# An attention and feed-forward layer on one core: weights read without copies, v's products in wider matmuls, and softmax sums over single tiles

## The chip, the cores and the metric

The kernel runs on one core of a Trainium2 chip. The metric is the device time of one execution in microseconds (us), lower is better. The median of three runs of the kernel before is 2360.73 us (2359.38 to 2362.85). A separate, profiled execution gives the trace that is read below.

## The reference

The layer works on x of 2 x 2048 rows with C = 1024 columns, all in float32:

```
x = x + attn(layernorm(x))        # one head of d = 256, keys over all 2048 rows
x = x + ffn(layernorm(x))

attn:  qkv = x @ Wqkv + bqkv;  p = softmax(q k^T / 16);  out = p v @ Wo + bo
ffn:   shared = relu(x @ up_w)^2 @ down_w                 # 1024 -> 2048 -> 1024
       routed = ((x @ fc1_w) @ expert_w) * (sum of the two largest of x @ gate_w) @ fc2_w
       layernorm(shared + routed) * gamma + beta
```

## The kernel before, in words

**Numbers.** Matmul operands are in a reduced float32 form. To keep accuracy, every operand is a pair: `hi`, the rounded value, and `lo`, what the rounding left. A product is three matmuls, hi x hi, lo x hi and hi x lo, added up in one PSUM tile (`Pass3`, L117 to L138, whose matmul is at L130). A split into hi and lo is a copy on ScalarE and a subtraction on VectorE (L142 and L143), now and then on GpSimd.

**Stages.** The 4096 rows are eight blocks of 512 rows, four for each batch element.

1. *Start* (`begin`, L458 to L520). `expert_w` is transposed on TensorE (tile `pt`, L480) and multiplied with `fc2_w` into the folded weight `fc2e` (tile `pf`). The first block of x is normalised and transposed on TensorE (L326) between the four quarters of the second of these products. The loads go through SyncE's queue.
2. *q, k and v* (`qkv_block`, L408). For each block come four v tiles (`v_tile`, L418: 128 rows x 256 columns, eight chunks of C, three matmuls each: tile `pv`) and four chunks of q and k (tile `pq`, 512 columns). Meanwhile the next block is normalised and transposed: a VectorE transpose of 32 x 32 tiles, a store to DRAM (`xt_d`), and a fetch in another order (`xt`), both on GpSimd's queue.
3. *Attention* (L712 to L763). For each of eight query blocks: scores of 16 key chunks (`ps`), the maximum, `softmax` (L581) in eight steps of two chunks, values (`po`), then `finish` (L611) and `project` (L632, tile `pw`). `softmax` adds the exponentials into a tile `sum` of 128 x 1024, two halves for the even and the odd chunks; `finish` sums over the 128 partitions and the two halves with matmuls of one column against a column of ones (tile `psum`, L622): four row tiles times two halves, 8 matmuls to a query block in the program. The trace shows each of them as two records, 16 to a query block and 128 in all.
4. *Feed-forward* (L1033 to L1290). For each of four pairs of blocks: 70 pieces of the up stage (`pu`) and 70 of the down stage (`pd`), in a scheme of seven products in place of eight (`p1` to `p7`), whose right sides are quarters of the weights or sums of quarters. A piece takes twelve matmuls. `stage` (L797) issues a piece's load on SyncE's queue into the second half of a tile `w`, `cast_piece` (L829) makes its hi on ScalarE, `end_piece` (L836) its lo on VectorE in place, and, for some pieces, stores the pair to DRAM (`w_p`, on GpSimd's queue), from where later blocks load it without a split. The pieces run about five ahead of their use; there are seven `w` tiles.

**Copies and sums of weights.** Sums of quarters are made by DMA alone: a copy of one quarter to a DRAM tile `wt` (L391), then accumulating DMAs (L399). `COPIES` lists 14 such copies: eight are the first terms of sums, six are plain copies of a quarter (three of `up_w`, three of `down_w`) so that all pieces come from tiles. `sum_step` issues one copy and perhaps one sum. It is called after blocks 4, 5 and 6 of the q, k and v stage, and at two points of each query block from the second on. A copy of a quarter with its part of `fc1_w` or `fc2e` is 2.5 MB.

**Order.** The start, the first seven q, k and v blocks and the feed-forward run in the order that the program writes (`manual_schedule`). For the eighth block and the attention a planner orders each engine's instructions by its own costs and by when their inputs are due; it may pull feed-forward instructions ahead into the end of the attention. `Norm(1)`, the second block's normalisation for the first pair, is spread over up pieces m = 0 to 13; its products `p4` start at m = 20.

Of the kernel before, what the change touches and what calls it, by code (L numbers as in the profile page):

```python
# [9 lines left out]
FP = mybir.dt.float32  # L10
# [15 lines left out]
def kernel(  # L26
# [353 lines left out]

    FIRST = {1: (0, 1), 2: (1, 1), 3: (0, 1), 4: (1, 0)}
    SUMS = [(s, q) for s in range(2) for q in (1, 3, 2, 4)]
    COPIES = SUMS + [(s, q) for s in range(2) for q in ((0, 0), (1, 0), (1, 1))]
    ADDS = dict(zip((4, 5, 6, 8, 9, 10, 11, 13), SUMS))
    last = [None]

    def sum_step(i):

        s, q = COPIES[i]
        for o, t in zip(sum_tile(s, q), quarter(s, *FIRST.get(q, q))):  # L390
            nc.gpsimd.dma_start(out=o, in_=t)  # L391
        if i in ADDS:
            s, q = ADDS[i]
            if q % 2:
                terms = quarter(s, *((0, 0) if q == 1 else (1, 1)))
            else:
                terms = sum_tile(s, q // 2)
            for o, t in zip(sum_tile(s, q), terms):
                nc.gpsimd.dma_start(out=o, in_=t, accum_op=ALU.add, max_dma_last_dim=4096)  # L399
# [8 lines left out]
    def qkv_block(n, wqkv, xT, parts, after):  # L408
# [9 lines left out]
        def v_tile(t):  # L418
            pm = bank(psa, "pv")
            if t % 2 == 0:  # L420
                got["v"] = half("v")
            acc = Pass3(pm[:, :D], NCC)
            for c in range(NCC):
                acc.add(x_chunk(xT, c, ts(t, P)), piece(wqkv[2], c, D, slice(0, D)))
            vt = got["v"][:, ts(t % 2, D)]
            nc.vector.tensor_tensor(vt, pm[:, :D], bv_sb, ALU.add)
            flush()
            split_late(vt, *(hl(units["v"])[:, s, ts(t, D)] for s in range(2)))
# [29 lines left out]
    def begin(wqkv, xT):  # L458
# [16 lines left out]

        eh, el = unit("eh"), unit("el")
        for mc in range(NLC):
            pt = bank(psc, "pt")
            for lc in range(NLC):
                nc.tensor.transpose(pt[:, ts(lc, P)], ew[:, ds(lc * LAT + mc * P, P)], ident)  # L480
            split(pt, eh[:, ts(mc, LAT)], el[:, ts(mc, LAT)])

# [25 lines left out]
        for t in range(NB):  # L508
            if t + 1 < NB:
                stats.append(row_stats(first[t + 1]))  # L510
            normalise(first[t], stats[t])
            if t == 0:
                f2hl = split_f2(1, nc.gpsimd)
            elif t == 2:
                wqkv[2] = split_unit(*ws[2], nc.gpsimd)
        r = [folded(0, accs)]
        r.append(folded(1, fold(f2hl, lambda t: transpose_tile(first[t], t, xT))))
# [63 lines left out]
    def softmax(n, j):  # L581

        s = st[n]
        s["p"].append(unit(f"p{n}_{j}"))
        e = s["s"][j // 2][:, ts(j % 2, C)]
        hi, lo = (hl(s["p"][j])[:, i, :] for i in range(2))
        e2 = e.rearrange("p (k n) -> p k n", n=W)
        mb = s["mb"].unsqueeze(1).to_broadcast([P, 2, W])
        nc.vector.tensor_tensor(e2, e2, mb, ALU.subtract)
        nc.scalar.activation(e, e, AF.Exp, scale=SC)  # L590
        split(e, hi, lo)
        if j == 0:
            s["e0"] = e
        elif j == 1:
            s["sum"] = row(f"sum{n}")
            nc.vector.tensor_tensor(s["sum"], s["e0"], e, ALU.add)
        else:
            nc.vector.tensor_tensor(s["sum"], s["sum"], e, ALU.add)
# [12 lines left out]
    def finish(n):  # L611
# [8 lines left out]
        for t in range(NB):  # L620
            for i in range(2):
                nc.tensor.matmul(  # L622
                    pt[:, t : t + 1],
                    lhsT=s["sum"][:, ds(i * W + t * P, P)],
                    rhs=ones,
                    start=i == 0,
                    stop=i == 1,
                )
# [63 lines left out]
    with tc.manual_schedule():  # L692
        norm, fold = begin(wqkv, xT)
        x3 = lambda: None
        steps = list(range(len(COPIES)))
        for i in range(NBLK - 1):
# [6 lines left out]
            if i >= NBLK // 2:  # L703
                sum_step(steps.pop(0))
# [81 lines left out]
    UPS = [up_order(4 if b == 0 else 1) for b in range(NBLK // 2)]  # L786
# [6 lines left out]
    def source(s, q, i):  # L793
        t, j = (tsum[s, q][0], i) if i < HU // P else (tsum[s, q][1], i - HU // P)
        return t[:, ts(j, P)].rearrange("(c p) i -> p c i", p=P) if s == 0 else t[ts(j, P), :]

    def stage():  # L797
# [3 lines left out]
        if len(pieces) < LATE and early:  # L801
            staged.append((early.pop(0), False, None))
            return
        n_w[0] += 1
        w = (wk if n_w[0] % 7 else wv).tile([P, 2 * W], FR, tag="w", name="w")
        if (s, p, i) in kept:
            nc.sync.dma_start(out=w.bitcast(FP), in_=kept[s, p, i])
            staged.append((w, False, None))
            return
        nc.sync.dma_start(out=as_piece(f32(w)[:, W : 2 * W], s), in_=source(s, RIGHT[p], i))  # L810
# [7 lines left out]
        staged.append((w, True, (s, p, i) if keep else None))  # L818
# [10 lines left out]
    def cast_piece():  # L829

        w, raw, key = staged.pop(0)
        if raw:
            nc.scalar.copy(w[:, 0:W], f32(w)[:, W : 2 * W])  # L833
        cast.append((w, raw, key))

    def end_piece():  # L836

        w, raw, key = cast.pop(0)
        if raw:
            v = f32(w)  # L840
            nc.vector.tensor_tensor(w[:, W : 2 * W], v[:, W : 2 * W], v[:, 0:W], ALU.subtract)  # L841
# [191 lines left out]
    with tc.manual_schedule():  # L1033
        for b in range(NBB):
# [72 lines left out]
            for m, (p, i) in enumerate(UPS[b]):  # L1107
# [229 lines left out]
```

## Time and profile before

| | |
|---|---|
| median of three runs | 2360.73 us |
| the profiled execution | 2357.94 us |
| its span on the core | 2355.8 us |
| TensorE matmul busy | 2323.3 us |
| VectorE busy | 1501.8 us |
| ScalarE busy | 1168.1 us |
| GpSimd busy | 285.4 us |
| moved by DMA | 572.54 MB, mean 243 GB/s |
| mean granted TensorE clock | 0.997 |

The span runs from the first to the last instruction. The profiled execution's own time is 2.1 us longer than its span, for what lies around it. A matmul's record lasts longer than the distance to the next one's start, since matmuls overlap; the distance is what counts against the time. Busy shares are averages over stages; which engine sets the time is read stage by stage.

| stretch, us | stage |
|---|---|
| 0 to 39.3 | start |
| 39.3 to 310.7 | q, k and v, eight blocks |
| 310.7 to 767 | attention |
| 767 to 2355.8 | feed-forward, four pairs |

### The profile page before, as it was taken

The numbers are of one execution on the slowest core, as the hardware profiler recorded it, in microseconds if no ns is written. First come the engines' busy times: TensorE is split into PE (matmuls) and PEld (weight loads), VectorE is DVE, ScalarE is ACT, GpSimd is POOL, SyncE is SP. The second block draws the span as 40 slices with busy tenths as digits, with TensorE's granted clock in tenths as the row PEclk, the third lists the DMA queues.
The fourth block names the chain that finished last, engine by engine and source line by source line (L and its number), as shares of the span: only waits on it lengthen the run. The fifth ranks groups of instructions, "written<-read, shape, count | busy, mean of one in ns | idle before, by whom it ended". The sixth has DMA issues, their size and how long they took to land.

```text
span 2355.8 us, 29360 instructions
## 1 busy us (share of the span) xinstructions
PE 2323.3 (99%) x10704; PEld 1919.4 (81%) x10704; DVE 1501.8 (64%) x2238; ACT 1168.1 (50%) x1916; POOL 285.4 (12%) x425
## 2 busy tenths in 40 slices
PE   8999999999999999999999999999999999999997
PEld 7888888888887778788788888878888877888886
DVE  5566559888877575797645577753456683435656
ACT  6555455555544643667552374743055564214245
POOL 3232111011110110111110011110000021000001
PEclk9999999999999999999999999999999999999999
DMA  5977884999997766786897789786567589665674
GB/s 197 318 256 276 286 205 127 296 315 323 286 253 211 250 208 191 228 276 209 265 316 242 229 297 319 229 267 227 193 204 278 194 267 331 189 191 187 204 247 134
DMA packets 222208, 572.54 MB, mean 243 GB/s; under 512 B 18368, under 2 KB 80320, under 8 KB 220016
## 3 DMA queue, kind: packets, MB, share of 16 engines
q1 hardware_dynamic: 152160, 315.67, 39.9%
q0 software_dynamic: 69904, 255.00, 36.1%
q8 instruction: 85, 1.39, 0.2%
q14 instruction: 59, 0.48, 0.1%
HBM read 430.61 MB, written 197.66 MB: 267 GB/s over the span
## 4 chain that ended last, share of the span: by engine, by line
PE 91%; DMA 3%; issue 3%; DVE 1%; ACT 1%; POOL 0%; SPq 0%; POOLq 0%; DVEq 0%; ACTq 0%
PE pu L130 31%; PE pd L130 28%; PE po L130 7%; PE pq L130 7%; PE ps L130 7%; PE pv L130 4%; PE pw L130 4%; DMA w<-wt 2%; PE pg L890 1%; PE pf L130 1%; PE psum L622 1%; DMA xt<-xt_d 0%; DVE w L841 0%; DMA ew<-in_L_ffn_expert_w_dram 0%; DMA res<-x 0%
## 5 line engine op out<-in xcount | busy, mean ns | idle before, releaser
L130 PE MATMUL pd<-w,sp 128*128 128x512 f32 x3336 | 759.0, 389 | 4.9 <-DVE y L1274 4.8
L130 PEld LDWEIGHTS pd<-w,sp 128*128 128x128 f32 x3336 | 625.5, 188 | 137.3 <-ACT nm L260 6.0
L130 PE MATMUL pu<-xh,w 128*128 128x512 f32 x2240 | 692.8, 390 | 0.1
L130 PEld LDWEIGHTS pu<-xh,w 128*128 128x128 f32 x2240 | 419.2, 188 | 89.9 <-DVE w L841 1.5
L130 PE MATMUL pu<-xl,w 128*128 128x512 f32 x1120 | 436.2, 389 | 0.9 <-DVE xl L150 0.9
L841 DVE TENSOR_TENSOR w<-w 128x512 fp32r<-128x512 f32 x280 | 191.6, 687 | 99.0 <-ACT w L833 92.0
L833 ACT CAST w<-w 128x512 fp32r<-128x512 f32 x280 | 170.9, 615 | 166.2 <-DMA w<-wt 155.6
L130 PEld LDWEIGHTS pu<-xl,w 128*128 128x128 f32 x1120 | 210.2, 188 | 45.1 <-DVE xl L150 1.4
L1077 ACT CAST sp<-h 128x512 fp32r<-128x512 f32 x238 | 146.3, 618 | 151.9 <-PE pd L130 125.6
L1082 DVE TENSOR_TENSOR sp<-h,sp 128x512 fp32r<-128x512 f32 x238 | 162.9, 687 | 68.1 <-ACT sp L1077 67.9
L130 PE MATMUL po<-p,v 128*128 128x512 f32 x768 | 194.3, 391 | 0.6 <-DVE p L143 0.6
L130 PE MATMUL ps<-q,k 128*128 128x512 f32 x768 | 192.5, 390 | 1.5 <-DVE max L565 1.5
L130 PEld LDWEIGHTS ps<-q,k 128*128 128x128 f32 x768 | 143.6, 188 | 31.8 <-DVE max L565 1.9
L130 PEld LDWEIGHTS po<-p,v 128*128 128x128 f32 x768 | 143.0, 188 | 30.2 <-DVE p L143 1.0
L150 DVE TENSOR_TENSOR xl<-xt,xh 128x512 fp32r<-128x512 f32 x108 | 74.4, 689 | 134.9 <-ACT xh L149 134.9
L1027 ACT ACTIVATE h<-h 128x1024 f32<-128x1024 f32 x48 | 50.7, 1055 | 208.8 <-DVE h L1137 159.8
L560 ACT COPY s<-ps 128x512 f32<-128x512 f32 x128 | 75.0, 587 | 133.5 <-PE ps L130 133.4
L213 DVE STREAM_TRANSPOSE xblk<-xrow 128x1024 f32<-128x1024 f32 x60 | 121.1, 2018 | 9.6 <-ACT xrow L283 9.6
L844 POOL DMA_DIRECT2D w_p<-w x115 | 61.6, 536 | 508.7 <-DVE w L841 435.0
L565 DVE TENSOR_TENSOR max<-ps,max 128x512 f32<-128x512 f32 x120 | 82.4, 687 | 36.3 <-ACT s L560 36.1
L130 PE MATMUL pq<-xha,w_h 128*128 128x512 f32 x256 | 99.7, 389 | 0.0
L130 PE MATMUL pq<-xha,w_l 128*128 128x512 f32 x256 | 99.7, 389 | 0.0
(181 smaller groups left out, 3031.8 us busy)
## 6 DMA issues: line engine op xcount, KB each, us to landing
w<-w_p SPq DMA_DIRECT2D x280, 512.0 KB, 4.2
w<-wt SPq DMA_DIRECT2D x280, 256.0 KB, 3.4
w_p<-w POOLq DMA_DIRECT2D x115, 512.0 KB, 4.6
xt_d<-xblk POOLq DMA_DIRECT2D x56, 512.0 KB, 4.4
xt<-xt_d POOLq DMA_DIRECT2D x56, 512.0 KB, 6.7
wt<-in_L_ffn_up_w_dram POOLq DMA_DIRECT2D x9, 2048.0 KB, 23.8
wt<-in_L_ffn_down_w_dram POOLq DMA_DIRECT2D x9, 2048.0 KB, 31.1
xres<-in_L_attn_x_dram SPq DMA_DIRECT2D x32, 512.0 KB, 11.2
```

The source lines that it names most:

```text
L130: nc.tensor.matmul(self.ps, lhsT=a, rhs=b, start=self.i == 0, stop=self.i == self.n - 1, skip_group_check=self.on,)
L150: late_ops.append(lambda: nc.vector.tensor_tensor(lo, t, f32(hi), ALU.subtract))
L213: nc.vector.transpose(b.rearrange("p (q k i) -> p q k i", q=P // SQ, i=SQ), r.rearrange("p (k i q) -> p q k i", k=NCC, i=SQ),)
L560: nc.scalar.copy(s["s"][k // 4][:, ts(k % 4, W)], pm)
L565: nc.vector.tensor_tensor(s["max"], pm, s["max"], ALU.max)
L622: nc.tensor.matmul(pt[:, t : t + 1], lhsT=s["sum"][:, ds(i * W + t * P, P)], rhs=ones, start=i == 0, stop=i == 1,)
L833: nc.scalar.copy(w[:, 0:W], f32(w)[:, W : 2 * W])
L841: nc.vector.tensor_tensor(w[:, W : 2 * W], v[:, W : 2 * W], v[:, 0:W], ALU.subtract)
L844: nc.gpsimd.dma_start(out=kept[key], in_=w.bitcast(FP))
L1027: nc.scalar.activation(o, v, AF.Relu)
L1077: nc.scalar.copy(t[:, 0:W], v)
L1082: add(t[:, W : 2 * W], v, f32(t)[:, 0:W], ALU.subtract)
```

## The change: what it does

- **v's weights side by side.** For each chunk of C the hi and lo columns of v's weights lie next to each other, 512 wide. One matmul multiplies x's hi by both, one of 256 columns x's lo by hi. VectorE adds the two halves of the PSUM tile, in one instruction more to a tile. The weights are split in two halves, one after the other, beside the second product of the start, with their subtraction on GpSimd.
- **Halves of sums.** In the last step of `softmax`, VectorE adds the two halves of `sum` and then the two halves of the last exponentials, so `finish` has one matmul to a row tile.
- **Fewer copies, sums in single terms.** The three quarters of `up_w` and `fc1_w` are no longer copied; their pieces load from the inputs, into a tile of the pool `spp` (`raw`), except for the first four pieces of `p1`, which come from a copy `lead` of 1 MB. `sum_step` issues one term, a copy or an accumulation: two in the start, 14 in the attention, one in the first up stage at m = 46. The copies of `down_w`'s three quarters move to m = 16, 26 and 36 of the first up stage. None is left in the q, k and v stage.
- **TensorE kept awake.** Transposes of the identity into an unused PSUM tile: 3 ahead of the first transposes, 14 ahead of the third group, 5 after the last.
- **An earlier second block.** The eleven steps of `Norm(1)` come at m = 0 to 11 in place of 0 to 13, and the splits for `p4` start at m = 11 in place of 13.

```diff
+    SECOND = {1: (0, 0), 2: 1, 3: (1, 1), 4: 2}
     SUMS = [(s, q) for s in range(2) for q in (1, 3, 2, 4)]
-    COPIES = SUMS + [(s, q) for s in range(2) for q in ((0, 0), (1, 0), (1, 1))]
-    ADDS = dict(zip((4, 5, 6, 8, 9, 10, 11, 13), SUMS))
+    LEAD = 4
+    STEPS = [(a, 0) for a in SUMS[:3]]
+    for a, c in zip(SUMS, SUMS[3:] + [None] * 3):
+        STEPS += ([(c, 0)] if c else []) + [(a, 1)]
+    STEPS.insert(3, None)
+    lead = dram.tile([HC, LEAD * P], FP, name="wt_lead")
...
     def sum_step(i):
+        if STEPS[i] is None:
+            nc.gpsimd.dma_start(out=lead, in_=up_w[0:HC, 0 : LEAD * P])
+            return
+        (s, q), second = STEPS[i]
+        a = (SECOND if second else FIRST)[q]
+        terms = quarter(s, *a) if isinstance(a, tuple) else sum_tile(s, a)
+        for o, t in zip(sum_tile(s, q), terms):
+            if second:
+                nc.gpsimd.dma_start(out=o, in_=t, accum_op=ALU.add, max_dma_last_dim=4096)
+            else:
+                nc.gpsimd.dma_start(out=o, in_=t)
+
+    def copy_step(q):
+        for o, t in zip(sum_tile(1, q), quarter(1, *q)):
             nc.gpsimd.dma_start(out=o, in_=t)
...
-            acc = Pass3(pm[:, :D], NCC)
             for c in range(NCC):
-                acc.add(x_chunk(xT, c, ts(t, P)), piece(wqkv[2], c, D, slice(0, D)))
+                xh, xl = x_chunk(xT, c, ts(t, P))
+                w = wqkv[2][c // 4].rearrange("p (c n) -> p c n", n=2 * D)[:, c % 4]
+                ops = [(pm, xh, w), (pm[:, :D], xl, w[:, :D])]
+                for i, (o, x_, w_) in enumerate(ops[:: 1 if c + 1 < NCC else -1]):
+                    nc.tensor.matmul(
+                        o,
+                        lhsT=x_,
+                        rhs=w_,
+                        start=c + i == 0,
+                        stop=c == NCC - 1 and i == 1,
+                        skip_group_check=True,
+                    )
             vt = got["v"][:, ts(t % 2, D)]
             nc.vector.tensor_tensor(vt, pm[:, :D], bv_sb, ALU.add)
+            nc.vector.tensor_tensor(vt, pm[:, D : 2 * D], vt, ALU.add)
...
+        def busy(n):
+            pt = bank(psb, "busy")
+            for _ in range(n):
+                nc.tensor.transpose(pt[:, 0:P], ident, ident)
+
         eh, el = unit("eh"), unit("el")
+        busy(3)
         for mc in range(NLC):
+            if mc == 2:
+                busy(14)
...
+        busy(5)
...
-            elif t == 2:
-                wqkv[2] = split_unit(*ws[2], nc.gpsimd)
         r = [folded(0, accs)]
-        r.append(folded(1, fold(f2hl, lambda t: transpose_tile(first[t], t, xT))))
+        wqkv[2] = []
+
+        def beside(t):
+            transpose_tile(first[t], t, xT)
+            if t < 2:
+                sum_step(steps.pop(0))
+            if t in (1, 2):
+                u = unit(f"w2_{t}")
+                uv = u.rearrange("p (c n) -> p c n", n=2 * D)
+                wv = ws[2][1].rearrange("p (c n) -> p c n", n=D)[:, ts(t - 1, NCC // 2)]
+                split(wv, uv[:, :, 0:D], uv[:, :, D : 2 * D], nc.gpsimd)
+                wqkv[2].append(u)
+
+        r.append(folded(1, fold(f2hl, beside)))
...
+        last = j == NKC // 2 - 1
+        if last:
+            half_sum = s["sum"][:, 0:W]
+            nc.vector.tensor_tensor(half_sum, half_sum, s["sum"][:, W:C], ALU.add)
         nc.vector.tensor_tensor(e2, e2, mb, ALU.subtract)
...
+        elif not last:
+            nc.vector.tensor_tensor(s["sum"], s["sum"], e, ALU.add)
         else:
-            nc.vector.tensor_tensor(s["sum"], s["sum"], e, ALU.add)
+            for i in range(2):
+                nc.vector.tensor_tensor(half_sum, half_sum, e[:, ts(i, W)], ALU.add)
...
         for t in range(NB):
-            for i in range(2):
-                nc.tensor.matmul(
-                    pt[:, t : t + 1],
-                    lhsT=s["sum"][:, ds(i * W + t * P, P)],
-                    rhs=ones,
-                    start=i == 0,
-                    stop=i == 1,
-                )
+            nc.tensor.matmul(
+                pt[:, t : t + 1], lhsT=s["sum"][:, ts(t, P)], rhs=ones, start=True, stop=True
+            )
...
-            if i >= NBLK // 2:
-                sum_step(steps.pop(0))
...
+    def direct(s, p, i):
+        return s == 0 and p in ("p1", "p2", "p3") and (p, i // LEAD) != ("p1", 0)
+
+    def source(s, p, i):
+        q = RIGHT[p]
+        if s == 0 and isinstance(q, tuple):
+            parts = quarter(s, *q) if direct(s, p, i) else [lead]
+        else:
+            parts = tsum[s, q]
...
-        nc.sync.dma_start(out=as_piece(f32(w)[:, W : 2 * W], s), in_=source(s, RIGHT[p], i))
+        if direct(s, p, i):
+            raw = spp.tile([P, 2 * W], FP, tag="sp", name="raw")[:, 0:W]
+        else:
+            raw = f32(w)[:, W : 2 * W]
+        nc.sync.dma_start(out=as_piece(raw, s), in_=source(s, p, i))
...
-                if b == 0 and m in (0, 1, 2, 4, 6, 8, 9, 10, 11, 12, 13):
+                if b == 0 and m in (0, 1, 2, 3, 4, 6, 7, 8, 9, 10, 11):
                     norm2.step()
...
+                if b == 0 and m in (16, 26, 36):
+                    copy_step(((0, 0), (1, 0), (1, 1))[m // 10 - 1])
+                elif b == 0 and m == 46:
+                    sum_step(steps.pop(0))
-                m4 = 12 if b == 0 else 10
+                m4 = 10
```

More of the change, by code (lines that the diff above doesn't have):

```diff
@@ L381 @@
     FIRST = {1: (0, 1), 2: (1, 1), 3: (0, 1), 4: (1, 0)}
+    SECOND = {1: (0, 0), 2: 1, 3: (1, 1), 4: 2}
     SUMS = [(s, q) for s in range(2) for q in (1, 3, 2, 4)]
-    COPIES = SUMS + [(s, q) for s in range(2) for q in ((0, 0), (1, 0), (1, 1))]
-    ADDS = dict(zip((4, 5, 6, 8, 9, 10, 11, 13), SUMS))
+    LEAD = 4
[4 more added lines that the diff above has]
+    lead = dram.tile([HC, LEAD * P], FP, name="wt_lead")
     last = [None]
     def sum_step(i):
-        s, q = COPIES[i]
-        for o, t in zip(sum_tile(s, q), quarter(s, *FIRST.get(q, q))):
-            nc.gpsimd.dma_start(out=o, in_=t)
[L392 to L399, printed above, removed]
+        if STEPS[i] is None:
[11 more added lines that the diff above has]
+        for o, t in zip(sum_tile(1, q), quarter(1, *q)):
+            nc.gpsimd.dma_start(out=o, in_=t)
     kv = {}
@@ L692 @@
     with tc.manual_schedule():
+        steps = list(range(len(STEPS)))
         norm, fold = begin(wqkv, xT)
         x3 = lambda: None
-        steps = list(range(len(COPIES)))
         for i in range(NBLK - 1):
@@ L784, in up_order @@
         return order + [(p, i) for p in ("p4", "p6", "p5", "p3", "p7") for i in range(NK)]
-    UPS = [up_order(4 if b == 0 else 1) for b in range(NBLK // 2)]
+    UPS = [up_order(LEAD if b == 0 else 1) for b in range(NBLK // 2)]
     DOWN = [(p, i) for p in ("p1", "p2", "p6", "p5", "p3", "p7", "p4") for i in range(NK)]
@@ L791 @@
     LATE = 5
-    def source(s, q, i):
-        t, j = (tsum[s, q][0], i) if i < HU // P else (tsum[s, q][1], i - HU // P)
+    def direct(s, p, i):
[6 more added lines that the diff above has]
+            parts = tsum[s, q]
+        t, j = (parts[0], i) if i < HU // P else (parts[1], i - HU // P)
         return t[:, ts(j, P)].rearrange("(c p) i -> p c i", p=P) if s == 0 else t[ts(j, P), :]
@@ L801, in stage @@
         if len(pieces) < LATE and early:
-            staged.append((early.pop(0), False, None))
+            staged.append((early.pop(0), None, None))
             return
@@ L807, in stage @@
             nc.sync.dma_start(out=w.bitcast(FP), in_=kept[s, p, i])
-            staged.append((w, False, None))
+            staged.append((w, None, None))
             return
-        nc.sync.dma_start(out=as_piece(f32(w)[:, W : 2 * W], s), in_=source(s, RIGHT[p], i))
+        if direct(s, p, i):
[3 more added lines that the diff above has]
+        nc.sync.dma_start(out=as_piece(raw, s), in_=source(s, p, i))
         if s == 1 and p in ("p3", "p7", "p4"):
@@ L817, in stage @@
             keep = b == 1 or i % 2 == 0
-        staged.append((w, True, (s, p, i) if keep else None))
+        staged.append((w, raw, (s, p, i) if keep else None))
     early, n_w = [], [0]
@@ L831, in cast_piece @@
         w, raw, key = staged.pop(0)
-        if raw:
-            nc.scalar.copy(w[:, 0:W], f32(w)[:, W : 2 * W])
+        if raw is not None:
+            nc.scalar.copy(w[:, 0:W], raw)
         cast.append((w, raw, key))
@@ L838, in end_piece @@
         w, raw, key = cast.pop(0)
-        if raw:
-            v = f32(w)
-            nc.vector.tensor_tensor(w[:, W : 2 * W], v[:, W : 2 * W], v[:, 0:W], ALU.subtract)
+        if raw is not None:
+            nc.vector.tensor_tensor(w[:, W : 2 * W], raw, f32(w)[:, 0:W], ALU.subtract)
         if key:
```

## The prediction

> **What bounds the kernel now.** I read the busy times first, then the chain of work that ended last, then the waits of TensorE, then single stretches.
>
> ```profile
> PE 2323.3 (99%) x10704; PEld 1919.4 (81%) x10704; DVE 1501.8 (64%) x2238; ACT 1168.1 (50%) x1916; POOL 285.4 (12%) x425
> PE 91%; DMA 3%; issue 3%; DVE 1%; ACT 1%; POOL 0%; SPq 0%; POOLq 0%; DVEq 0%; ACTq 0%
> ```
>
> The second line should not be trusted alone, and neither should 99%: matmul records overlap. So I took the distance from each matmul's start to the next one's: their sum is 2338.5 us; 3.7 us lie before the first matmul and 13.6 us after the last one's start, which makes the span of 2355.8. Taking the usual distance for each kind (227 ns for 512 columns, 120 ns for 256) leaves some 26 us of the 2338.5 as stalls. TensorE's instruction stream sets the time almost everywhere, so an instruction taken from TensorE counts in full, and one put on another engine counts only where that engine is late. The waits of TensorE say where:
>
> ```profile
> PE pt L480 <- DMA ew<-in_L_ffn_expert_w_dram: 7.2, 2, 3.7
> PE pd L130 <- DVE y L1274: 4.8, 3, 2.0
> PE pv L130 <- ACT xha L142: 2.2, 1, 2.2
> PE ps L130 <- DVE max L565: 1.5, 1, 1.5
> ...
> PE pu L130 <- DVE xl L150: 0.9, 1, 0.9
> ```
>
> (us in total, times, longest). Nothing here is large; the change can win little from waits and must win from instruction count.
>
> **1. The sums of softmax.** In the chain in order of time, these are v and q/k of one block, and the sums of one query block (start, us, what):
>
> ```profile
> 39.43 11.51 PE pv L130 x96
> 50.94 21.79 PE pq L130 x96
> ...
> 436.18 1.68 PE psum L622 x16
> ```
>
> Sixteen records take 1.68 us, 105 ns each, on TensorE's path eight times. Half go: 8 x 0.84 = **6.7 us off**. In exchange VectorE gets a 512-wide add for the halves (about 0.69, from the 512-wide `max` rows) and two 512-wide adds in place of one of 1024 (2 x 0.61 against 1.14 start to start), some 0.8 us per query block. In the steady state VectorE is busy about eight tenths and the last add is six steps of values ahead of `finish`: nothing. In the last query block, where no scores run, VectorE is full:
>
> ```profile
> 745.00:755.00 10.00, 10.00 (x46) 8.28 (x45) 10.00 (x11) 5.50 (x7) 4.07 (x6) 1.00 1.04 285
> ```
>
> (us, TensorE, its weight loads, VectorE, ScalarE, GpSimd, clock, DMA share, GB/s) and the timeline has, at its end:
>
> ```profile
> 756.69 1.23 DVE L598 TENSOR_TENSOR sum<-sum,s 128x1024 f32<-128x1024 f32 x1 [0.53 <-ACT s L590]
> 757.83 1.22 DVE L143 TENSOR_TENSOR p<-s,p 128x1024 fp32r<-128x1024 f32 x1
> ...
> 759.14 1.84 PE L622 MATMUL psum<-ones,sum 128*128 128x1 f32 x16
> ```
>
> The sum ends at 757.9 and is used at 759.14: 1.2 us to spare. TensorE comes 0.84 us earlier (the block before has lost its sums too) and VectorE 0.8 us later: 0.4 us late, and `p`'s lo behind it as much. I count **0.6 us lost**, bounded by 0 (the planner fills in up-stage matmuls, as it does at 756.64) and 1.6.
>
> **2. v's products.** A 256-column matmul costs 11.51/96 = 119.9 ns, a 512-column one 21.79/96 = 227.0. Three of the first become one of each: 359.7 becomes 346.9, 12.8 ns off, times 8 chunks x 32 tiles: **3.3 us off**. The added VectorE instruction is 0.41 us (the row of L426) times 32; VectorE works 154.8 of 271 us in this stage and four PSUM banks stand between it and TensorE: nothing. Its weights are ready in time: ScalarE's two halves (half of 1.92 us each) follow the transposes of tiles 1 and 2 at about 30 and 34 us, GpSimd's two subtractions (half of 4.62 us) end near 33.5 and 37, v starts at 39.3. If that cover of 2 us were gone it would cost what it is late.
>
> **3. Awake.** The first products run at half clock:
>
> ```profile
> 9.11 1.94 PE L480 MATMUL pt<-ident,ew 128*128 128x128 f32 x8 [3.49 <-DMA ew<-in_L_ffn_expert_w_dram]
> 12.24 0.79 PE L130 MATMUL pf<-f2h,eh 128*128 128x512 f32 x1 [1.19 <-ACT f2h L142]
> 13.69 0.63 PE L130 MATMUL pf<-f2h,eh 128*128 128x512 f32 x1
> 15.95 0.39 PE L130 MATMUL pf<-f2h,eh 128*128 128x512 f32 x1
> ```
>
> From 12.24 to 15.4 the distance is 0.43 us in place of 0.227, 7 times, and 0.36 more at the first: 1.8 us. The granted clock turns full at 15.6. With a full clock before 12 the transposes of the last groups are quicker too, and 0.2 us could come from there: 2.0 at most. The 22 added transposes at 0.21 us fit: 14 take 3.0 us of the 3.5 us wait, 5 take 1.1 of the 1.2 before 12.24. Against it stands the Trainium skill, TensorE: Matmul & The Clock Gate, Part 4 (PE-mode transpose): full clock does not engage for transposes, which do not count as busy in the same way. By that rule the gain is 0. The row of eight transposes (1.94 us in the last 3.1 us before the matmuls) did not raise the clock, but it filled too little of the time to decide. I take the middle, **1.0 us off**.
>
> **4. The pair's second block, earlier.** At 831.7 the first matmul of `p4` with a lo waits 1.1 us for `xl` (the wait of 0.9 above and its start-up). Its split comes two pieces, 5.4 us, earlier, and the eleven normalisation steps with their SyncE row loads, VectorE transposes and GpSimd stores and fetches too, into a stretch where ScalarE works 6.0 to 6.5 of 10 us, out of one (805 to 815) where it works 9.9: **1.1 us off**.
>
> **5. Copies and sums.** They are DMAs from GpSimd's queue, and cost only through what they delay. The price of a pair (2.5 MB): in the stage of q, k and v the `q_d` store issued at 204.4 lands after 9.1 us, at 213.5, and the pair issued behind it lands after 14.6 and 15.7, at 221.2. So 8 us by itself; the Trainium skill, DMA: Bandwidth & Descriptors (Queues, rings and completion order), adds that an engine consumes one ring in order and takes turns between the rings of several queues. So SyncE's loads lose half their rate while a copy lasts, and GpSimd's own transfers wait for all of it. By the page's limit of memory, 358 GB/s for a core, 5.2 MB read and written would take 15 us. I use the row, 8 us, where little else runs, and 15 where other loads run.
>
> *In the start*, two pairs are issued at about 26 to 29 us, behind GpSimd's 6 us of `f2l`. SyncE has some 2 MB to come; `w1` lands near 40 instead of 33 and its split on ScalarE starts at 41.9. The copies end near 29 + 16 + 6 = 51; the first `xt_d` is issued at 52.35, so it and the fetches behind it lose 0 to 3 us (by the page's rate the copies end near 64: see the second rival). The last fetch of a block lands 0.4 us after the next block begins and is used three v tiles, 8.6 us, later. Nothing.
>
> *In the eighth block* TensorE stalls at 278.0 for `xha`, with a slower clock behind it: 5.0 us in excess of the usual distances. The last fetch was issued at 270.5 and took 7.7 us (4.4 in the block before). The removed copy of the sixth block had landed by 254.5, so the delay comes from SyncE's own loads of `q_d` and `Wo`, which stay: 0, up to 5.0 off if I misread this.
>
> *In the attention* there are fewer transfers; they were hidden.
>
> *In the first up stage* three pairs and one accumulated pair are put ahead of `w_p` stores. A store is issued two pieces ahead of use (of which a piece is 2.72 us), its tile's next load five pieces ahead of a use seven later. Behind a 15 us copy issued at m = 16, the store of piece 20 lands at about m = 22.3; the load of piece 27 wants the tile at m = 22. Loads here took up to 9.3 us without a stall over 0.3. Nothing.
>
> *Direct pieces* load as many bytes in the same 512-byte runs; `raw` frees the load from waiting for `w`, ScalarE's copy waits for it instead, one piece later. The fifth load must wait for the memory of v's last units (about 752 us), where the kernel before issued five loads from 705.6 on; SyncE's queue holds fetches of x and residual loads at 730 to 743, which I expect the planner to put ahead. Nothing; 5 to 11 us lost if it does not.
>
> **Sum.** -6.7 + 0.6 - 3.3 - 1.0 - 1.1 = -11.5 us. Against the profiled execution's 2357.94 that is 2346.4; the median of the runs lies 2.8 us above it, so **2349.2 us**, 0.49% less. This kernel's runs tell a change from none at about 0.2%, 4.7 us.
>
> **The rivals.**
>
> *The eighth block's stall goes too.* For it: a 2.5 MB copy was in that queue in each of the three blocks. Against: landed by 254.5. Time: 2349.2 - 5.0 = 2344.2. Chance 0.10.
>
> *Late tiles in the second and third block.* The start's copies, then the fold's stores and the next rows, keep GpSimd's queue late until a fetch lands over 3 us late, as in the eighth block. Each such block costs its 5.0: 2354.2 to 2359.2. For it: the margin of 1 us at 52.35. Chance 0.12.
>
> *SyncE held by the fifth load.* Four x fetches and four residual loads issued at 752 to 756 instead of 730 to 743 leave TensorE with some values and two PSUM banks of projection: 5 to 11 us, near 2357. Against: readiness is what the planner orders by. Chance 0.06.
>
> *VectorE becomes the bound of the attention.* If every query block loses the added 0.7 us, 5.6 go: 2354.8. Against: two tenths idle. Chance 0.03.
>
> *Slower: stores behind copies.* In the attention such copies and sums took 31 to 45 us to land. If one takes 31 us in the up stage, the store of piece 20 lands at m = 28, the load of 27 comes at 28 and its split at 29.7: 2.7 pieces, 7.4 us late, in each of three copies, and as much for the sum: 30 - 11.5, 2368. It decides from about 20 us of holding on. Against: DMA is 0.66 busy here, 0.90 in the attention. Chance 0.08.
>
> **How the numbers follow.** The forecast has 0.61: 2345 to 2353 (the bounds of part 3, and of the last query block). Faster by over 0.2%, under 2356: the forecast, the first rival, half of the second, most of the third, the fourth, 0.82. Slower by over 0.2%, over 2365.4: 0.09, the last rival and a little for two at once. Within: 0.09. The range 2342 to 2358 leaves out the slow rival and the second's worse half, and a little below.
>
> **What would show it.** `psum` x64 and 0.84 us in each row of the chain; `pv` with 256 matmuls of 512 columns, 11.1 us a block; full clock by 12 us or again at 15.6; no wait for `xl` at the start of `p4`; the wait for `xha` at about 265. Wrong, if TensorE waits for `xt`, for `w` in pieces 27 to 35, or for x near 757.

## The result and the profile after

The kernel became slower: 2377.85 us (median of six runs, 2374.69 to 2382.04) against 2361.36 us of the kernel before beside it (six runs, 2358.23 to 2362.94). The ratio is 1.0073, with a 95% interval of 1.0060 to 1.0086. The prediction was 2349.2 us. The profiled execution took 2374.69 us, with a span of 2372.9 us, 17.1 us more than before.

The page of the changed kernel, its busy times and its chain by engine:

```profile
PE 2323.3 (98%) x10406; PEld 1902.8 (80%) x10406; DVE 1520.5 (64%) x2286; ACT 1167.5 (49%) x1917; POOL 281.0 (12%) x421
PE 78%; DMA 8%; issue 5%; DVE 4%; ACT 2%; POOL 1%; SPq 1%; POOLq 0%; DVEq 0%; ACTq 0%
```

TensorE has 298 records fewer, as foreseen, and DMA went from 3% to 8% of the chain. The waits of TensorE (us in total, times, longest):

```profile
PE ps L130 <- DVE max L610: 10.9, 2, 10.6
PE pd L130 <- DVE y L1335: 4.8, 3, 1.7
PE pu L130 <- DVE w L898: 4.7, 3, 3.1
PE pv L439 <- ACT xha L142: 4.6, 2, 4.3
PE pu L130 <- ACT w L891: 3.2, 1, 3.2
...
PE pq L130 <- DVE v L449: 1.4, 2, 1.3
```

Four new or larger waits stand out: one of 10.6 us for the maximum of the scores, two for weights in the up stage (3.2 and 3.1), one of 4.3 us at the last block of q, k and v. The next table puts each at its place. It takes the start of one kind of matmul in both traces as a mark, and lists how much later (+) or earlier (-) it comes after the change.

| stretch, by the start of | time in before, us | gained or lost, us |
|---|---|---|
| span's start to the first block's q and k | 0 to 50.8 | -2.0 |
| to the third block's q and k | to 117.4 | +2.1 |
| to the seventh block's q and k | to 250.6 | -0.6 |
| to the eighth block's q and k | to 288.7 | +1.9 |
| to the sixth query block's `psum` | to 665.4 | -4.7 |
| to the seventh query block's `psum` | to 724.7 | +10.9 |
| to piece 4 of the up stage | to 783.0 | -1.6 |
| to piece 30 | to 862.0 | +1.9 |
| to piece 60 | to 943.8 | +9.9 |
| to the end | to 2355.8 | -0.6 |
| sum (unrounded) | | +17.1 |

The gains on TensorE are there. Two losses, of 11 and 10 us, outweigh them.

**The loss in the attention.** The timelines of SyncE's queue, ScalarE, VectorE and TensorE in the changed kernel show the wait of 10.6 us and what ended it (start, us, what, idle time before it and what ended that):

```profile
701.43 11.45 SPq L868 DMA_DIRECT2D w<-wt_lead  x4
...
716.84 0.62 ACT L891 CAST w<-w 128x512 fp32r<-128x512 f32 x1 [14.81 <-DMA w<-wt_lead]
717.37 0.58 ACT L605 COPY s<-ps 128x512 f32<-128x512 f32 x1
...
718.10 0.68 DVE L610 TENSOR_TENSOR max<-ps,max 128x512 f32<-128x512 f32 x1
...
718.84 2.93 PE L130 MATMUL ps<-q,k 128*128 128x512 f32 x6 [10.63 <-DVE max L610]
```

Beside these loads GpSimd's queue moves a copy and a sum of weights; the sum was issued at 689 us and its larger part lands 29 us later. The first load of 256 KB of feed-forward weights takes 15.4 us, the other three about 20. The first piece that uses such a load starts at 758.7 us, but the planner has put its copy to hi (L891) into ScalarE's stream ahead of the copy of a score tile (L605), so the attention waits for it. Around these waits TensorE's granted clock falls too (stretch, TensorE busy, its loads, VectorE, ScalarE, GpSimd, clock, DMA share, GB/s):

```profile
713.00:723.00 10.00, 4.16 (x10) 3.29 (x11) 3.21 (x4) 3.35 (x6) 0.00 (x0) 0.50 0.93 209
...
938.00:948.00 10.00, 6.39 (x14) 4.73 (x15) 4.23 (x7) 7.69 (x11) 0.53 (x1) 0.51 0.48 156
```

**The loss in the up stage.** The timeline there shows the accumulation that is issued at m = 46, and what a piece then waits for:

```profile
916.54 1.96 POOL L404 DMA_DIRECT2D wt<-wt  x2
...
937.85 0.62 ACT L891 CAST w<-raw 128x512 fp32r<-128x512 f32 x1 [18.49 <-DMA raw<-in_L_ffn_up_w_dram]
938.52 0.80 PE L130 MATMUL pu<-xh,w 128*128 128x512 f32 x1 [3.20 <-ACT w L891]
...
942.40 0.79 PE L130 MATMUL pu<-xh,w 128*128 128x512 f32 x1 [3.09 <-DVE w L898]
```

**Why a load of 256 KB takes 13 to 20 us.** A "packet" is here what the profile counts as one: a run of 512 or of 4096 bytes in these loads and sums. The DMA view of the changed kernel for 918 to 936 us (packets, MB, share of the 16 engines' time; then issues with the median us to landing):

```profile
DMA packets 1623, 4.01 MB, mean 223 GB/s; under 512 B 78, under 2 KB 729, under 8 KB 1622
...
q0 software_dynamic: 952, 3.66, 94.9%
q1 hardware_dynamic: 670, 0.33, 8.2%
...
raw<-in_L_ffn_up_w_dram SPq DMA_DIRECT2D x4, 256.0 KB, 16.0
...
wt<-wt POOLq DMA_DIRECT2D x1, 512.0 KB, 19.6
```

and of the kernel before for the same stretch of time, where no sum runs:

```profile
q1 hardware_dynamic: 3652, 1.81, 34.4%
q0 software_dynamic: 359, 1.34, 20.9%
...
w<-wt SPq DMA_DIRECT2D x6, 256.0 KB, 3.1
```

The engines are full, and SyncE's queue (q1) gets 0.33 of 4.01 MB: 8%, not half. The packet counts tell why. A piece of weights is read in runs of 512 bytes, 512 packets a load; the accumulation (q0) moves packets of 4096 bytes. In part of the stretch q1 moves nothing. From 925 to 933 us both queues have work all the time:

```profile
q0 software_dynamic: 363, 1.42, 94.5%
q1 hardware_dynamic: 354, 0.18, 11.3%
```

That is one packet of each in turn, and 11% of the bytes for q1. In the attention, from 706 to 718 us, the counts are 585 and 585. From the shares, a packet of q0 holds an engine 0.945 x 16 x 8 / 363 = 0.33 us, one of q1 0.113 x 16 x 8 / 354 = 0.041 us. 354 packets in 8 us make 11.6 us for the 512 of a load. Before that a load waits for its turn to begin: the one issued at 921.00 us moves its first packet 3.5 us later, where one of the kernel before (issued at 924.76) needs 1.0 us. That load took 16.8 us. A piece is used every 2.72 us, and five pieces of lead, 13.6 us, don't cover it. What is shared evenly is turns, not bytes.

### The profile page after: what moved, and what is told of

The parts are those of the page before. It is cut to its first block, busy times and chain, and to the rows that moved or that the text cites. A ratio compares the mean times of both kernels' runs of the same rounds, so it can differ in the third digit from the quotient of the medians.

```text
span 2372.9 us, 28742 instructions
## 1 busy us (share of the span) xinstructions
PE 2323.3 (98%) x10406; PEld 1902.8 (80%) x10406; DVE 1520.5 (64%) x2286; ACT 1167.5 (49%) x1917; POOL 281.0 (12%) x421
## 4 chain that ended last, share of the span: by engine, by line
PE 78%; DMA 8%; issue 5%; DVE 4%; ACT 2%; POOL 1%; SPq 1%; POOLq 0%; DVEq 0%; ACTq 0%
PE pu L130 30%; PE pd L130 28%; PE po L130 7%; PE ps L130 7%; PE pw L130 4%; DMA w<-wt 2%; DMA xt_d<-xblk 2%; DVE xblk L213 1%; PE pg L947 1%; DMA w<-in_L_attn_Wqkv_dram 1%; PE pq L130 1%; DMA w<-wt_lead 1%; DMA raw<-in_L_ffn_up_w_dram 1%; DVE xla L143 1%; DMA xt<-xt_d 1%
## 5 line engine op out<-in xcount | busy, mean ns | idle before, releaser
L891 ACT CAST w<-w 128x512 fp32r<-128x512 f32 x241 | 147.2, 615 | 153.3 <-DMA w<-wt 115.1
L898 DVE TENSOR_TENSOR w<-w 128x512 fp32r<-128x512 f32 x241 | 164.9, 686 | 89.3 <-ACT w L891 85.3
L130 PE MATMUL ps<-q,k 128*128 128x512 f32 x768 | 193.9, 392 | 10.9 <-DVE max L610 10.9
L130 PEld LDWEIGHTS ps<-q,k 128*128 128x128 f32 x768 | 144.3, 189 | 41.9 <-DVE max L610 11.8
L605 ACT COPY s<-ps 128x512 f32<-128x512 f32 x128 | 74.8, 585 | 133.3 <-PE ps L130 133.2
```

Source lines behind the costliest of these rows:

```text
L130: nc.tensor.matmul(self.ps, lhsT=a, rhs=b, start=self.i == 0, stop=self.i == self.n - 1, skip_group_check=self.on,)
L605: nc.scalar.copy(s["s"][k // 4][:, ts(k % 4, W)], pm)
L891: nc.scalar.copy(w[:, 0:W], raw)
L898: nc.vector.tensor_tensor(w[:, W : 2 * W], raw, f32(w)[:, 0:W], ALU.subtract)
```

## The experiments

**1. The accumulation at m = 46 in small packets.** If turns are what counts, packets of 512 bytes in the accumulation give SyncE's loads a much larger share.

```diff
-    def sum_step(i):
+    def sum_step(i, width=4096):
...
-                nc.gpsimd.dma_start(out=o, in_=t, accum_op=ALU.add, max_dma_last_dim=4096)
+                nc.gpsimd.dma_start(out=o, in_=t, accum_op=ALU.add, max_dma_last_dim=width)
...
-                    sum_step(steps.pop(0))
+                    sum_step(steps.pop(0), 512)
```

> Theory (turns): the 16 DMA engines take one packet from SyncE's ring and one from GpSimd's by turns, so a load in 512-byte packets behind an accumulation in 4096-byte packets (0.33 us each) is slow because of the size of the other's packet. With the accumulation of m = 46 cut into 512-byte packets, the loads beside it land in under 8 us (13 to 17 in the changed kernel), the wait at pieces 56 and 57 of the first up stage (3.4 + 3.7 us and a half clock behind it) goes, and the piece 50 to 60 stretch gives back 9 to 10 us: about 2368. Rival (amount): what counts is the 2.5 MB that run beside the loads, or the loads wait for the whole transfer: nothing gained, about 2378, or slower as small packets last longer.

Its DMA view for 918 to 938 us, and then the queues alone for 930 to 938 us, where both have work all the time:

```profile
q0 software_dynamic: 3735, 2.81, 83.4%
q1 hardware_dynamic: 2977, 1.48, 32.5%
...
wt<-wt POOLq DMA_DIRECT2D x1, 2048.0 KB, 22.2
...
raw<-in_L_ffn_up_w_dram SPq DMA_DIRECT2D x4, 256.0 KB, 9.1
```

```profile
q0 software_dynamic: 1588, 0.81, 79.4%
q1 hardware_dynamic: 1578, 0.78, 50.1%
```

The packets are again one to one, and with equal sizes the bytes are too: 0.81 and 0.78 MB. The loads land after 9.1 us instead of 16.0, with the same bytes to move beside them. The packet sizes, not the bytes, set the loads' share. The gain was half of what was expected: from piece 50 to piece 60 the loss falls from 9.8 to 4.5 us. The loads took 9.1 us where under 8 was expected, and the sum itself lasted 22 to 25 us, for 17 to 20. The total hardly moved: 2376.92 us (four runs, 2373.31 to 2381.66; ratio 1.0075, 1.0059 to 1.0092), where 2368 was expected; in this profile other stretches lost more than in the changed kernel's (1.2 us between pieces 30 and 40, 2.2 before the eighth block's q and k). So the mechanism is shown and its gain in the total is not.

**2. The accumulation moved to the down stage.** There the pieces are read in runs of 2048 bytes. The rival was that direct reads of the inputs are slow by themselves.

```diff
-                elif b == 0 and m == 46:
-                    sum_step(steps.pop(0))
...
                         down(t, s, w)
+                    if b == 0 and (j, k) == (0, 2):
+                        sum_step(steps.pop(0))
```

> The step of m = 46 is issued in the first down stage, at the third piece. A down piece is as many bytes, 256 KB, but in 2048-byte rows, a quarter of the packets. Theory (turns): its loads land in under 9 us beside the accumulation, within the cover of five pieces, and the 9.8 us are gone: about 2368. Rival (amount): loads wait for the accumulation as before, and the stall of some 10 us moves to the down stage: about 2378. Rival (direct reads): the loads straight from the up weights are slow by themselves; then pieces 56 and 57 still wait with no accumulation beside them, and about 2378.

Pieces 50 to 60 lose nothing (+0.02 us): direct reads are not slow by themselves. But the loss came back in the down stage: 8.9 us by its twentieth piece. Its DMA view for 1000 to 1024 us:

```profile
q0 software_dynamic: 1390, 5.24, 81.5%
q1 hardware_dynamic: 837, 1.80, 22.7%
...
w<-wt SPq DMA_DIRECT2D x8, 256.0 KB, 6.2
...
xrow<-x SPq DMA_DIRECT2D x1, 512.0 KB, 14.1
```

SyncE's share rose to 1.80 of 7.04 MB, with larger packets, as turns demand (from 1007 to 1013 us the counts are 244 and 244, the bytes 1.00 and 0.46 MB). I had left out that the row loads of a normalisation go through the same queue: a row of 512 KB and four pieces, 1.5 MB, stood behind each other, and the last two pieces landed after 15 and 16 us. The expected 2368 us was wrong. The total was 2380.8 us (1.0091, 1.0076 to 1.0106). Of the profile's time 9.8 us are lost by the second block's q and k, 7.0 of them in one wait in the first block's; that belongs to the start's copies (experiment 5).

**3. No step in the last query block.** The steps that the changed kernel issues there go ahead into earlier query blocks.

```diff
-            if k in (2, 8) and n > 1 and steps:
+            if n > 1 and steps and (k in (2, 8) if n < NBLK else False) or k == 5 and n in (2, 3):
```

> The same steps, but none in the last query block: the two that stood there are issued one each at a further point of the second and third. Theory: the first four loads of the up stage, which the planner puts into the attention at about 700 us, land in 6 to 7 us, ScalarE's copies behind them are held 5 us and not 15, and TensorE's wait of 10.8 us with a half clock behind it becomes one of 1 to 2 us: 11 to 12 us less, about 2366. Rival (planner): the wait comes from where the planner put ScalarE's copies of weights, ahead of the scores' copies, and stays at 8 us or more though the loads come early: about 2375.

The timeline then has the same loads and casts without the wait (the loads land after 3.6 us in the median):

```profile
703.13 2.02 SPq L868 DMA_DIRECT2D w<-wt_lead  x4
...
705.93 0.62 ACT L891 CAST w<-w 128x512 fp32r<-128x512 f32 x1 [2.20 <-DMA w<-wt_lead]
707.02 1.52 PE L130 MATMUL ps<-q,k 128*128 128x512 f32 x6
```

The stretch from the sixth to the seventh `psum` is 2.7 us shorter than before the change instead of 10.9 longer: 13.6 us come back. The total is 2364.25 us (13 runs; ratio 1.0019, 1.0011 to 1.0028). By the ratios, more than half of the slowdown was two steps issued too late in the attention. The kernel before issues three of its 14 in the q, k and v stage, so the attention's places, two to a query block, are used up before the last one, and none stands beside these loads.

**4. TensorE's parts alone.** The kernel before with v's weights side by side, the halves added by VectorE and TensorE kept awake; its copies and sums stay.

> The kernel before with the three parts that touch TensorE's instructions alone (v's weights side by side, halves of sums, transposes of the identity in the start); all copies and sums of weights, direct loads and the normalisation stay as before. By the traces: 0.91 us less in each of eight query blocks, 0.26 in each of eight blocks of v, 1.75 in the start: 11.1 less than before, about 2350. Rival: the added VectorE work or the planner's new order costs part of it: 2355 or more.

```diff
+                ops = [(pm, xh, w), (pm[:, :D], xl, w[:, :D])]
...
+            nc.vector.tensor_tensor(vt, pm[:, D : 2 * D], vt, ALU.add)
...
+        busy(3)
...
+        if last:
+            half_sum = s["sum"][:, 0:W]
```

2357.74 us against 2359.89: ratio 0.9997 (0.9986 to 1.0009), no difference, where the prediction counts these parts at -10.4 us and the expectation above at -11.1. The rival's side was right. By marks the gains were -1.3 us in the start, -0.26 in each q, k and v block and -0.9 in each query block. They were given back at waits: 2.9 us at the eighth block and 2.2 at the sixth query block's `psum` (residual rows in GpSimd's queue that took 30 us), both ended by a transfer; 2.1 for `w` early in the second pair and 2.4 after it, whose causes weren't traced. The waits of TensorE and, in the DMA view of 266 to 282 us, what the first of them stands for:

```profile
PE pv L427 <- ACT xha L142: 5.5, 1, 5.5
...
PE ps L130 <- DVE max L596: 3.3, 2, 1.9
```

```profile
xrow<-in_L_attn_Wo_dram SPq DMA_DIRECT2D x2, 512.0 KB, 6.8
xt<-xt_d POOLq DMA_DIRECT2D x1, 512.0 KB, 8.3
...
xrow<-q_d SPq DMA_DIRECT2D x1, 512.0 KB, 9.5
```

The last fetch landed at 278.8 us, against 278.2 before, while TensorE came 2.9 us earlier; the wait grew by about that.

**5. The start without copies.** The two steps of the start come after the fifth and sixth block of q, k and v (i = 4 and 5), where the kernel before had its own.

```diff
-            if t < 2:
-                sum_step(steps.pop(0))
...
+            if i in (4, 5):
+                sum_step(steps.pop(0))
```

> The changed kernel without the two steps in the start; they are issued after the fifth and sixth block of q, k and v, where the kernel before had such copies too. Theory (turns): the load of k's weights lands at about 33 us and not at 43 to 49, ScalarE does not wait for it, v's PSUM banks come free in time, and the 1.3 us or more at the first q and k chunks and the smaller stalls of the next blocks go: the second block's q starts 1.9 us before that of the kernel before and not 0.7, and by the fifth block 2.7 us before it: 3 to 4 us less than the changed kernel, about 2374. Rival: ScalarE's order (weights' split ahead of v's) holds the banks anyway: no more than 1 us less.

2373.69 us, ratio 1.0047 (1.0033 to 1.0060): about 4 us less than the changed kernel by the medians, 6 by the ratios. In its trace the loss at the second and third blocks is gone (-0.26 at each, from +1.3 and +0.8), but later blocks then wait a little for theirs and 2.8 us are lost at the eighth. In the changed kernel k's weights landed at 43.2 us, after 22 us, instead of 33.0; in the profile of experiment 2 at 48.7. From the first block's q and k to the third's, with the own gains of these blocks, the start's copies cost 2.6 us in the changed kernel, 2.7 in experiment 1's profile, 3.5 in experiment 3's and 10.1 in experiment 2's.

**6. The eighth block.** To experiment 4 one edit is added: the q rows and `Wo`, which SyncE loaded beside the last fetch, go to GpSimd's queue behind it.

```diff
-                    start(0, load_row(q_d[0]))
+                    with tc.issue_after(fetched[0].ins):
+                        q0 = load_row(q_d[0], nc.gpsimd)
+                    start(0, q0)
...
-    wo_f = [load_row(Wo[ts(dc, P), :]) for dc in range(NDC)]
+    with tc.issue_after(fetched[0].ins):
+        wo_f = [load_row(Wo[ts(dc, P), :], nc.gpsimd) for dc in range(NDC)]
```

> The kernel before with the three TensorE parts, and the loads of q's rows and Wo in the eighth block on GpSimd's queue behind the last fetch of x, not beside it on SyncE's. Theory: the gain of v and of the start (4 us by the eighth block) is given back there since the last fetch lands at 278 to 279 whatever TensorE does; with nothing beside it, the fetch lands some 4 to 6 us earlier, and the eighth block's q and k start 4 to 6 us before those of the TensorE parts alone: about 2352. Rival: the fetch is late by its own chain of stores and fetches; then nothing, about 2358.

In the same view the fetches now land after 4.8 us, and the loads that were in their way after 20, when nobody waits for them yet:

```profile
xt<-xt_d POOLq DMA_DIRECT2D x2, 512.0 KB, 4.8
xrow<-q_d POOLq DMA_DIRECT2D x2, 512.0 KB, 19.3
xrow<-in_L_attn_Wo_dram POOLq DMA_DIRECT2D x2, 512.0 KB, 20.7
```

The stall of 5.5 us is gone. 2352.67 us, ratio 0.9957 (0.9943 to 0.9970): 10.3 us less than the kernel before beside it, where experiment 4 showed no difference. That the prediction's count for these parts was 10.4 is luck: 5 us of the 10.3 come from the stall that the kernel before has too, and other gains are lost again (in the profile 3.7 us at a late fetch for the seventh block, which the kernels below don't show, and 5.3 at the sixth query block's `psum`).

**7. All repairs together.** The changed kernel with experiments 3 and 5, part 4 of the change taken back, and the last sum issued in four quarters of rows at m = 44, 47, 50 and 53.

```diff
+                nc.gpsimd.dma_start(
+                    out=o[ts(r, 256), :], in_=t[ts(r, 256), :], accum_op=ALU.add,
+                    max_dma_last_dim=4096,
+                )
...
-                elif b == 0 and m == 46:
-                    sum_step(steps.pop(0))
+                elif b == 0 and m in (44, 47, 50, 53):
+                    sum_chunk(steps[0], (m - 44) // 3)
```

> The changed kernel with four things mended: the start's steps after the fifth and sixth block; none in the last query block; the normalisation of the second block where it was; the last sum in four parts of a quarter each at m = 44, 47, 50 and 53. Theory (turns): 3 to 4 us, 11 to 13 us, 2 to 3 us and 9 to 10 us less than the changed kernel's 2378, about 2349 to 2352, 8 to 11 less than before. Rival (amount): the parts of the last sum together still stall 5 us or more: 2355.

2354.04 us (six runs; ratio 0.9965, 0.9953 to 0.9977), faster than the kernel before, though above the expected 2349 to 2352. With the edit of experiment 6 added:

> The same, and the eighth block's loads of q's rows and Wo on GpSimd's queue behind the last fetch. Theory: 3 to 6 us less than the run with four things mended, about 2346. Rival: the loads come too late for the first scores instead and TensorE waits for q there: no gain.

2347.24 us (five runs, 2346.40 to 2349.35; ratio 0.9936, 0.9924 to 0.9949), the best version, 15.7 us below the kernel before beside it. Its waits include:

```profile
PE pd L130 <- DVE y L1351: 4.6, 2, 3.3
...
PE pu L130 <- DVE w L914: 2.2, 1, 2.2
```

From piece 50 to 60 it loses 0.01 us (1.5 without the edit of experiment 6): a quarter of the sum lands after 8.9 us, before five pieces have passed. It is 5.4 us faster than experiment 6's kernel, which keeps all copies. The two traces don't show one cause for that: this kernel has neither the late fetch nor the loss at the sixth query block's `psum`, and it loses 4.0 us between pieces 10 and 20 of the first up stage, where the kernel before loses nothing. The wait of 2.2 us for `w` lies there. It ends at 812.1 us, before the copy at m = 16 is issued (813.2); ahead of it ScalarE had stood still for 4.3 us for a direct load of `fc1_w`, which took 9.3 us beside GpSimd's fetches of x. No run takes that loss away.

**8. Part 4 alone.** The kernel before with the second block's earlier normalisation; and the same put back into the best version.

```diff
-                if b == 0 and m in (0, 1, 2, 4, 6, 8, 9, 10, 11, 12, 13):
+                if b == 0 and m in (0, 1, 2, 3, 4, 6, 7, 8, 9, 10, 11):
...
-                m4 = 12 if b == 0 else 10
+                m4 = 10
```

> The kernel before with part 4 of the change alone (the second block's eleven steps at m = 0 to 11, its splits for p4 from m = 11); everything is computed. The prediction's part 4: the wait of 0.9 us for xl at the start of p4 and its start-up go, -1.1 us between u0.20 and u0.30, and nothing comes in its place. The rival: the steps' row loads and GpSimd's stores and fetches come closer together and delay the loads of the pieces between m = 4 and m = 20, so that a wait for w of 1 to 2 us takes its place and the sum from u0.4 to u0.30 is between 0 and +1. In both the total stays within 2 us of before.

The waits of TensorE from 770 to 835 us:

```profile
PE pu L130 <- ACT xh L149: 0.7, 1, 0.7
PE pu L130 <- DVE w L841: 0.2, 1, 0.2
```

In before this stretch had one wait, 0.9 us for `xl`. Between pieces 20 and 30 the early steps win 1.27 us, as predicted to 0.2; between pieces 4 and 20 they lose 1.44, the larger part at a wait for `xh` that ends at 786.5 us, since ScalarE runs from 781.8 to 785.9 us the second pass of one row (L271), a table load of 1.28 us (L272) and the first pass of the next (L259) with nothing between, and the cast of `xh` stands behind them; in before a cast of `xh` came between at 783.7. The rival had the place and the size, but expected the wait at `w`. The total is 2360.29 against 2359.97 us, ratio 1.0000 (0.9991 to 1.0009).

> The best version so far (2347.2 us) with part 4 of the change put back in; everything is computed. There the later schedule of the kernel before left a wait of 2.4 us for w at 809.5 and one of 1.1 us for xl at 819.3, +4.0 us between u0.10 and u0.20. If the earlier schedule is the better one where pieces are loaded directly, u0.4 to u0.30 costs about 1.9 us as it did in the changed kernel, so 2 us less, about 2345. If those waits come from the direct loads and from the copy at m = 16 whatever the schedule, the time stays at 2347.

2347.66 us, ratio 0.9948 (0.9932 to 0.9964), the same as the best version within either interval, although its trace has 2.0 us less between pieces 4 and 30. So no preference can be measured.

## Why the prediction was wrong

**Part 5, copies and sums, is the step that failed.** It said that "SyncE's loads lose half their rate while a copy lasts". A load of 256 KB takes 3.1 us in the quiet stretch of before, so half a rate makes 6 us, well inside five pieces. The Trainium skill, DMA: Bandwidth & Descriptors (Queues, rings and completion order), which the prediction named there, says that an engine takes turns between rings at the granularity of a packet. I turned that into half of the bytes without asking how large the packets of either queue are. The trace of before had both sizes: loads in 512-byte runs, accumulations in 4096-byte ones. One packet of each in turn (363 and 354 from 925 to 933 us, so the trace agrees with the page) left SyncE 11% of the bytes and stretched a load to 15 to 20 us, where half a rate makes 6. Two sentences then fell with it:

- "In the attention there are fewer transfers; they were hidden." Fewer, but the steps, two in the start and 14 here, last until the final query block, where the loads for the up stage are already under way. The steps of before had run out by then. +11.8 us (10.9, and the gain of 0.9 that it hides); experiment 3 took it back.
- "Loads here took up to 9.3 us without a stall over 0.3. Nothing." That measured five pieces of cover against the loads of before. Beside the copies at m = 16, 26 and 36, which last 12 to 15 us, loads took up to 14 us and the cover held just about; beside the sum at m = 46, which lasts 16 to 20 us, it didn't. +9.8 us; experiment 7 took it back.

*In the start* the prediction saw w1 land near 40 us and its split start at 41.9, and counted nothing. It landed at 43.2, ScalarE waited 3.1 us for it, and TensorE lost 2.6 us between the first block's q and k and the third's.

**That "an instruction taken from TensorE counts in full"** failed as well. Parts 1 to 3 alone gave nothing in the total (experiment 4), so even with part 5 at nothing the sum of -11.5 us would not have come. The eighth block was read rightly in its cause: the loads of `q_d` and `Wo`, not the removed copy, delayed the last fetch (experiment 6). What was overlooked is that a stall set by a transfer takes back every gain made ahead of it: parts 2 and 3 won 2.9 us up to there in experiment 4, and lost them there.

**Part 1** was right: 0.91 us per query block for the predicted 0.84. From the seventh query block's `psum` to piece 4, where two sums at 0.91 lie, 1.6 us were gained: some 0.3 us were lost at the end, for the 0.6 counted.

**Part 2** was right in kind and too large: 0.26 us a block, 2.1 in all, for 3.3. Matmuls of 512 and of 256 columns that alternate start 236 + 118 = 354 ns apart, not 346.9; the sum took the spacing of the 512-column ones from q and k, where all are alike.

**Part 3** was too small: the first block's products began 1.75 us earlier, for 1.0. The first products of the fold ran at the full clock:

```profile
11.39 0.50 PE L130 MATMUL pf<-f2h,eh 128*128 128x512 f32 x1 [0.65 <-ACT f2h L142]
12.53 0.39 PE L130 MATMUL pf<-f2h,eh 128*128 128x512 f32 x1
```

In before the record of the same kind took 0.79 us at 12.24 and 0.39 only from 15.95 on. TensorE ran nothing but transposes up to then, and the first full-speed record of the granted clock lies at 6.3 to 9.2 us in the ten traces with the added transposes, at 15.6 and 16.6 us in the two without (the kernel before and experiment 8's first). So the rule of the Trainium skill, TensorE: Matmul & The Clock Gate (Part 4: PE-mode transpose), that transposes don't bring the full clock, doesn't hold for these float32 transposes. The middle between rule and bound was a wrong choice; the bound of 2.0 was nearer.

**Part 4** came to nothing for the 1.1 counted, by a wait that took the place of the one removed: -1.27 and +1.44 us (experiment 8).

**The rivals.** The slow one gave 2368 us by stores behind copies in the first up stage. The side was right and the place half right, but the mechanism was not: the stores' tiles were not what TensorE waited for, the loads were, and half of the loss lay in the attention. Neither the fifth load nor VectorE became a bound; in place of late tiles in the second and third block, k's weights were late in the first.

**What stays open.** The stretches add up to the 17.1 us of the two traces, and experiments 3, 5, 6 and 7 take its large parts away one by one. The cost of the start's copies differs from run to run for a reason that wasn't looked into. Pieces 10 to 20 lose 1.7 us in the changed kernel beyond what part 4 alone costs there, and 4.0 in the best version; whether the direct loads or their order in ScalarE's stream cause it isn't shown. Pieces 30 to 50, beside the copies at m = 26 and 36, lose up to 1.5 us in some profiles and nothing in others; these copies weren't moved alone. No run moved the casts of weights in ScalarE's stream, so what that order costs without late loads isn't measured.

## What to carry to other kernels

Before a transfer is called hidden, count the packets of each queue that works beside it: here the two queues took turns by packets, so small packets beside large ones got a small part of the bytes. Then issue the load earlier by the time that its packets need at that pace (11.6 us for 256 KB here, and 3.5 to begin), or cut the large transfer, as the best version does. Look also at what ScalarE does for a late load: a copy placed early in its stream made the attention wait, which didn't need the load at all. And a gain on the bounding engine counted only up to the next wait whose end a transfer sets; find that wait, and repair it with the same change.

## What the hardware showed that was not expected

- Transposes in float32 brought TensorE's clock up: full speed at 6.3 to 9.2 us for 15.6 and 16.6 without the added ones, and first fold products of 0.50 and then 0.39 us a record, for 0.79 before.
- A wait of TensorE cost more than itself: the clock of 0.50 reached 4.4 us past the end of the wait in the attention (718.8 to 723.2). Around the two short waits of 3.2 and 3.1 us in the up stage it lasted from 938.3 to 948.5 us, 6 us past the end of the second.
- While both queues had work, GpSimd's and SyncE's packets alternated one to one, with 512, 2048 or 4096 bytes a packet (363 and 354, 585 and 585, 1588 and 1578, 244 and 244 packets in four stretches). With sums in packets of 512 instead of 4096 bytes SyncE's queue got 49% instead of 11% of the bytes, and its loads took 9.1 instead of 16.0 us.
- An accumulation's packet of 4096 bytes held an engine 0.33 us, one of 512 bytes 0.064 us (0.794 x 16 x 8 / 1588); a load's packet of 512 bytes 0.041 us beside either.
